# Layer 2's last norm: mean and variance summed by ACT instead of DVE's statistics

## The chip, the cores and the metric

One NeuronCore of a Trainium2 chip runs the whole program. The metric is the device time of one execution in microseconds; lower is better. The engines are PE (matrix products, with its weight loads shown apart as PEld), DVE (vector), ACT (scalar and activation), POOL (GpSimd) and SP (which here issues all transfers).

## The reference

64 matrices of 256 x 128 pass through four layers. All share one 256 x 256 adjacency matrix, and each layer ends with the same residual norm:

```
def _layernorm(x, axis=-1, eps=1e-5):
    m = jnp.mean(x, axis=axis, keepdims=True)
    v = jnp.var(x, axis=axis, keepdims=True)
    return (x - m) / jnp.sqrt(v + eps)
...
x = _layernorm(x + _L0_gnn_ref(...))   # 5 gated steps: adj @ h, three gates, h updated
x = _layernorm(x + _L1_gnn_ref(...))   # two products with weights, mixed by a softmax over the edges
x = _layernorm(x + _L2_gnn_ref(...))   # attention over adj, norm, adj @ h, two-layer MLP with a norm
x = _layernorm(x + _L3_gnn_ref(...))   # Chebyshev: powers of adj times x times weights
```

Layer 2 has norms inside; the one this document is about is its last, over `x + relu(mlp + gat)`: for each of the 256 x 64 rows the mean and variance of 128 numbers, then `(x - m) * (v + eps)^-0.5`. Everything is fp32.

## The kernel before

The 64 matrices are worked in 32 *pairs*. A pair's activations are one tile of 128 partitions x 512: four blocks of 128 tokens x 128 features ("four tiles" of a norm are these blocks, `tokens(v)[:, c, :]`). Products with the adjacency are "spreads" (`spread`, L542, plain; `spread7`, L553, with seven block products in place of eight, whose sums DVE or POOL make at L572 to L574, L581, L585, L587). Between a spread and a weight product the tile may have to be turned (tokens against features): `turn` (L514) does it either by DVE's 32 x 32 transpose and a round trip through DRAM (L529, L531, L537), or by four PE transposes (L523) and a copy out of PSUM. Which of the two is taken is set per site by `BY_DMA` (L18): the last so many pairs of a site are turned by PE.

The order of work is not written out by hand. Every operation is added to a `Schedule` (L102) with the engines it may run on ("ways", each with an assumed duration), what it reads and what it writes. `order` (L132) then plans all 32 pairs at once, greedily: of all operations that are ready it takes the one that can start first, and among those the one that is latest against its due time; for an operation with several ways it takes the engine on which it would end first, after adding a handicap per engine from `SPARE` (L49). Tiles come from fixed classes with a count each (`CLASSES`, L41): a value gets a tile when its first operation is planned, and an operation that finds none free waits. So a change of one assumed duration, one handicap or one count reshuffles the orders of all engines.

The norms are of two sorts. `scale_norm` (L672), used where the mean is already zero, sums the squares by ACT (L645, `Square` with `accum_out`) or by DVE's bn_stats and bn_aggr (L639, L641). `layer_norm` (L626), used at the end of layers 0 and 2, needs mean and variance: `stats` (L591) gets both from DVE's bn_stats and bn_aggr (L600, L602), POOL adds eps and takes the power -0.5 (L605, L608), DVE makes minus mean times that (L610), and `normalize` (L613) applies both, half by half, on DVE (L617) or ACT (L622).

In layer 2 the last steps are: the turn of z, `products` with w2 (L721) on top of a bank seeded with the residual, `y = max(t, 0) + x2` on DVE (L810), `layer_norm(y, x2)` (L812). Layer 3 then turns the result (L529 and on) and spreads it, L827 and L828 multiply both by the weights, L835 multiplies one half by the squared adjacency, L645 to L667 make the last norm, and the result goes out (L841). `x_N` in the profile are the tiles that hold a pair's x through all layers.

Of the kernel before, what the change touches and what calls it, by code (L numbers as in the profile page):

```python
# [8 lines left out]
AF = mybir.ActivationFunctionType  # L9
ALU = mybir.AluOpType  # L10
# [4 lines left out]
D = 128  # L15
STEPS = 5

BY_DMA = {"h": 1, "y": 2, "x1": 0, "x2": 2, "w": 0, "z": 3, "x3": 0}  # L18

WARM = 4  # L20

# [16 lines left out]
ROWS = ["l1_bias", "bp", "b1", "gat_g", "gat_b", "b2"]  # L38


CLASSES = {"X": (512, 15), "T": (512, 4), "A": (512, 30), "H": (520, 6), "B": (1024, 6), "S": (32, 64), "PS": (512, 8), "D": (512, 4), "E": (1024, 8)}  # L41

SEEN = {"PE": 0.23, "ACT": 0.16, "DVE": 0.16, "POOL": 0.12, "SP": 0.0}

# [1 line left out]

AGAIN = {"DVE": 0.12, "POOL": 0.12}

SPARE = {"DVE": 1.0, "DVE+": 0.0, "POOL": -0.3}  # L49


DUE, LAST_DUE, LAST = 15.0, 12.0, 12
# [49 lines left out]
class Schedule:  # L102
# [29 lines left out]
    def order(self, tiles):  # L132
# [14 lines left out]
        while ready:  # L147
            best = None
            for op in ready:
# [7 lines left out]
                for engine, us, fn in op.ways:  # L157
                    us = us if engine == "PE" else us * MARGIN
                    start = max(op.ready, held, *(engines[e] for e in USES.get(engine, (engine,))))
                    end = start + us + SPARE.get(engine, 0.0)  # L160
                    if way is None or end < way[0]:
# [41 lines left out]
def kernel(ctx: ExitStack, tc: tile.TileContext, x, xT, adj, adjT, mats, cols, rows, out):  # L203
    nc = tc.nc
# [5 lines left out]
    S = Schedule(n_pairs)  # L210
# [7 lines left out]
    def act(us, fn, r, w):  # L218
        S.add([("ACT", us, fn)], r, w)

    def dve(us, fn, r, w):
        S.add([("DVE", us, fn)], r, w)
# [4 lines left out]
    def pool(us, fn, r, w):  # L227
        S.add([("POOL-", us, fn)], r, w)
# [103 lines left out]
    for it in range(2):  # L332
        dve(TT, lambda it=it: nc.vector.tensor_tensor_scan(cum.at(2, N)[:, it, :], ones.ap, edge.at(2, N)[:, it, :], 0.0,
                                                            op0=ALU.mult, op1=ALU.add), [edge, ones], [cum])
# [11 lines left out]
    for it in range(2):  # L346
        dve(0.45, lambda it=it: nc.vector.scalar_tensor_tensor(
            num.at(2, N)[:, it, :], cum.at(2, N)[:, it, :], first()[:, it:it + 1], edge.at(2, N)[:, it, :],
            op0=ALU.add, op1=ALU.mult), [cum, small, edge], [num])
        dve(0.35, lambda it=it: nc.vector.tensor_scalar(rowk.at(2, N)[:, it, :], kf.ap, last()[:, it:it + 1], None,  # L350
                                                        op0=ALU.is_lt), [kf, small], [rowk])
        dve(0.45, lambda it=it: nc.vector.scalar_tensor_tensor(
            rowk.at(2, N)[:, it, :], kf.ap, first()[:, it:it + 1], rowk.at(2, N)[:, it, :],
            op0=ALU.is_ge, op1=ALU.mult), [kf, small, rowk], [rowk])
# [13 lines left out]
    for kt in range(2):  # L368
        dve(0.4, lambda kt=kt: nc.vector.tensor_scalar(colk.at(2, N)[:, kt, :], t1.at(2, N)[:, kt, :], kc.ap[:, kt:kt + 1], None,
                                                       op0=ALU.is_equal), [t1, kc], [colk])  # L370
# [7 lines left out]
    for kt in range(2):  # L378
        dve(0.4, lambda kt=kt: nc.vector.tensor_scalar(erow.at(2, N)[:, kt, :], t2.at(2, N)[:, kt, :], col(f"e{kt}"), None,
                                                       op0=ALU.mult), [t2, ccol], [erow])  # L380
# [18 lines left out]
    for it in range(2):  # L399
        act(0.7, lambda it=it: nc.scalar.activation(lg.at(2, N)[:, it, :], lg.at(2, N)[:, it, :], AF.Exp,  # L400
                                                    bias=nmax()[:, it:it + 1], accum_out=den()[:, it:it + 1]), [lg, small], [lg, small])
    dve(0.2, lambda: nc.vector.reciprocal(den(), den()), [small], [small])
    dg = fixed([2, P], "dg")
    for it in range(2):
        blk = lambda it=it: lg.at(2, N)[:, it, it * P:(it + 1) * P]
        dve(0.35, lambda it=it: nc.vector.tensor_scalar(lg.at(2, N)[:, it, :], lg.at(2, N)[:, it, :], den()[:, it:it + 1], None,
                                                        op0=ALU.mult), [lg, small], [lg])
# [95 lines left out]
    def tokens(v):  # L503
        return v.at(4, D)
# [6 lines left out]
    def by_dma(site):  # L511
        return S.pair < n_pairs - BY_DMA[site]

# [74 lines left out]
                                                blk(sv, 0)[:, None, :].to_broadcast([P, 2, P])), [t, p1], [o])  # L588
        return o

    def stats(y, eps=None):  # L591

        s = Value("S", name="mv")
        mv = lambda: s.at(32)[:, 0:8].rearrange("p (t k) -> p t k", k=2)
        rs = lambda: s.at(32)[:, 8:12]
        st = Value("S", name="st")

        def fn():
            for c in range(4):
                nc.vector.bn_stats(st.at(4, 6)[:, c, :], tokens(y)[:, c, :])  # L600
            for c in range(4):
                nc.vector.bn_aggr(mv()[:, c, :], st.at(4, 6)[:, c, :])  # L602
        dve(1.07, fn, [y], [st, s])
        if eps is None:
            pool(0.23, lambda: nc.gpsimd.tensor_scalar(rs(), mv()[:, :, 1], LN_EPS, None, op0=ALU.add), [s], [s])  # L605
        else:
            pool(0.23, lambda: nc.gpsimd.tensor_tensor(rs(), mv()[:, :, 1], eps.at(4), op=ALU.add), [s, eps], [s])
        pool(1.02, lambda: nc.gpsimd.tensor_tensor(rs(), rs(), neg_half.ap, op=ALU.pow), [s, neg_half], [s])  # L608
        nmr = lambda: s.at(32)[:, 12:16]
        dve2(0.08, lambda: nc.vector.scalar_tensor_tensor(nmr(), mv()[:, :, 0], -1.0, rs(), op0=ALU.mult, op1=ALU.mult), [s], [s])  # L610
        return s, rs, nmr

    def normalize(y, o, s, rs, nmr):  # L613
        for half in ((0, 1), (2, 3)):
            def by_dve(half=half):
                for c in half:
                    nc.vector.tensor_scalar(tokens(o)[:, c, :], tokens(y)[:, c, :], rs()[:, c:c + 1], nmr()[:, c:c + 1],  # L617
                                            op0=ALU.mult, op1=ALU.add)

            def by_act(half=half):  # L620
                for c in half:
                    nc.scalar.activation(tokens(o)[:, c, :], tokens(y)[:, c, :], AF.Identity, bias=nmr()[:, c:c + 1],  # L622
                                         scale=rs()[:, c:c + 1])
            S.add([("ACT", 0.78, by_act), ("DVE" if y.cls == "PS" else "DVE+", 0.52, by_dve)], [y, s], [o])

    def layer_norm(y, o):  # L626
        normalize(y, o, *stats(y))

    def scale_stats(ts, eps=None):

# [46 lines left out]
    def layer0(x0, hT):  # L677
        h = x0
        for s in range(STEPS):
            mT = spread7(h, aT, aT7) if s in FAST and FIRST <= S.pair < n_pairs - FINAL else to_sbuf(spread(h, aT), "mT")  # L680
            t = bank()

            def reset(t=t, hT=hT, mT=mT):
                nc.tensor.matmul(t.at(512), mat("u3"), hT.at(512), start=True, stop=False)  # L684
                nc.tensor.matmul(t.at(512), w4.ap, mT.at(512), start=False, stop=True)  # L685
            pe(mm(1024), reset, [Wg, w4, hT, mT], [t])
            r, z, new = (Value("A", name=n) for n in ("r", "z", "hT"))
            act(0.59, lambda t=t, r=r: nc.scalar.activation(r.at(512), t.at(512), AF.Tanh, bias=bzrh.ap[:, 1:2], scale=0.5),  # L688
                [t, bzrh], [r])
            dve2(TT, lambda r=r, hT=hT: nc.vector.scalar_tensor_tensor(r.at(512), r.at(512), 1.0, hT.at(512),  # L690
                                                                      op0=ALU.add, op1=ALU.mult), [r, hT], [r])
            pe(mm(512), lambda t=t, mT=mT: nc.tensor.matmul(t.at(512), w3.ap, mT.at(512), start=False, stop=True,  # L692
                                                            skip_group_check=True), [w3, mT, t], [t])
            act(0.59, lambda t=t, z=z: nc.scalar.activation(z.at(512), t.at(512), AF.Tanh, bias=bzrh.ap[:, 0:1], scale=0.5),  # L694
                [t, bzrh], [z])
            t = bank()

            def candidate(t=t, mT=mT, r=r):
                nc.tensor.matmul(t.at(512), w5.ap, mT.at(512), start=True, stop=False)  # L699
                nc.tensor.matmul(t.at(512), u5h.ap, r.at(512), start=False, stop=True)  # L700
            pe(mm(1024), candidate, [w5, u5h, mT, r], [t])

            act(0.59, lambda t=t: nc.scalar.activation(t.at(512), t.at(512), AF.Tanh, bias=bzrh.ap[:, 2:3]), [t, bzrh], [t])  # L703
            dve(TT, lambda t=t, hT=hT: nc.vector.tensor_sub(t.at(512), t.at(512), hT.at(512)), [t, hT], [t])
            dve(TT, lambda t=t, z=z: nc.vector.scalar_tensor_tensor(t.at(512), z.at(512), 1.0, t.at(512),  # L705
                                                                   op0=ALU.add, op1=ALU.mult), [t, z], [t])
            dve(TT, lambda t=t, hT=hT, new=new: nc.vector.scalar_tensor_tensor(
                new.at(512), t.at(512), 0.5, hT.at(512), op0=ALU.mult, op1=ALU.add), [t, hT], [new])
            hT = new
            h = turn(hT, "h", "h" if s < STEPS - 1 else "y")  # L710
        y = Value("A", name="y")
        dve2(TT, lambda: nc.vector.tensor_add(y.at(512), h.at(512), x0.at(512)), [h, x0], [y])
        layer_norm(y, x0)

    def products(lefts, rights, t=None):

# [25 lines left out]
    def layer2(x2):  # L742
        xT = turn(x2, "xT", "x2")
        h = Value("H", name="h2")
        hs = lambda: h.at(4, D + 2)
        for b in range(2):
            t = Value("PS", name="ps")

            def fn(b=b, t=t):
                for i in range(2):  # L750
                    nc.tensor.matmul(t.at(2, D + 2)[:, i, :], tokens(xT)[:, 2 * b + i, :], wpx.ap, start=True, stop=True)  # L751
# [5 lines left out]
        u, s = Value("B", name="u"), Value("S", name="nm")  # L757
# [7 lines left out]
        for c in range(4):  # L765
            dve2(0.35, lambda c=c: nc.vector.tensor_tensor_reduce(
                out=u.at(4, N)[:, c, :], in0=sd.at(2, N)[:, c // 2, :], in1=maskb.ap[:, c % 2, :], scale=1.0, scalar=-NEG_MASK,
                op0=ALU.add, op1=ALU.max, accum_out=nm()[:, c:c + 1]), [sd, maskb], [u, s])
# [5 lines left out]
        for c in range(4):  # L774
            act(0.4, lambda c=c: nc.scalar.activation(u.at(4, N)[:, c, :], u.at(4, N)[:, c, :], AF.Prelu,
                                                       bias=hs()[:, c, D:D + 1], alpha=0.2), [u, h], [u])
        for c in range(4):
            act(0.5, lambda c=c: nc.scalar.activation(u.at(4, N)[:, c, :], u.at(4, N)[:, c, :], AF.Exp,
                                                       bias=nm()[:, c:c + 1], accum_out=den()[:, c:c + 1]), [u, s], [u, s])
        for b in range(2):  # L780
            half = lambda b=b: u.at(4, N)[:, 2 * b:2 * b + 2, :]
# [5 lines left out]
        for b in range(2):  # L787
# [15 lines left out]
        t, z = seed((0.49, 0.61), tokens, lambda: row("b1", 4), [rbc, gT]), Value("A", name="z")  # L803
# [4 lines left out]
        t, y = seed((0.49, 0.61), tokens, lambda: tokens(hb), [hb, zT]), Value("A", name="y")  # L808
        products([zT], [lambda: mat("w2")], t)
        dve(TT, lambda t=t: nc.vector.scalar_tensor_tensor(y.at(512), t.at(512), 0.0, x2.at(512), op0=ALU.max, op1=ALU.add),  # L810
            [t, x2], [y])
        layer_norm(y, x2)  # L812

    def layer3(x3, p):
        xT = turn(x3, "xT", "x3")
# [37 lines left out]
    tiles = {}  # L853
    for cls, (n, count) in CLASSES.items():
        where = {"PS": psum, "D": dram, "E": dram}.get(cls, shared)
# [46 lines left out]
```

## Time and profile before

| | |
|---|---|
| median of 4 runs | 1487.67 us (1487.22 to 1487.75) |
| the profiled execution | 1487.75 us |
| its span, first to last instruction | 1486.0 us |
| granted PE clock | 1.000 |
| transfers | 146 GB/s on average, 70.8% of 16 engines' time |
| instructions | 28119 |

The profiled execution's own time is 1.75 us longer than its span. How to read the rows: a group's row gives line, engine and operation, output and inputs by the program's tile names, shapes and count, then the busy time in us and the mean ns of one, then how long the engine had been idle before them and what ended the wait. [...]neighbours overlap, so what an operation occupies is the distance between two starts. fp32 matmuls leave two MATMUL records each, transposes one.

### The profile page before, as it was taken

How to read it: one execution, taken by the hardware profiler on the slowest of the kernel's cores; microseconds unless marked ns; L12 is line 12 of the kernel's file. 1: busy time of each engine (PE TensorE's matmuls, PEld its weight loads, DVE VectorE, ACT ScalarE, POOL GpSimd, SP SyncE). 2: the span in 40 equal slices, each digit the busy share in tenths (PEclk: the TensorE clock that was granted, in tenths of full speed). 3: DMA queues.
4: the chain of work that ended last, by engine and by line, in shares of the span. 5: the costliest groups of instructions: out<-in, count | busy, mean ns of one | idle time of the engine just before them, and what ended most of it. 6: DMA issues, size and time to landing. Idle time of an engine off the chain costs nothing.

```text
span 1486.0 us, 28119 instructions
## 1 busy us (share of the span) xinstructions
PE 1475.4 (99%) x7704; PEld 1063.3 (72%) x7704; DVE 1235.9 (83%) x3083; ACT 1027.7 (69%) x3116; POOL 831.1 (56%) x1307
## 2 busy tenths in 40 slices
PE   9999999999999999999999999999999999999998
PEld 6556666666676677777767677777676776788997
DVE  7767888988999899888888888878888888989872
ACT  3444556677777687876786767676686767878875
POOL 4512444555576776664556556565454746676542
PEclk9999999999999999999999999999999999999999
DMA  8544465777788988886778668777777776667862
GB/s 239 121 84 100 100 133 122 144 149 151 157 155 167 177 172 170 160 161 132 150 149 179 133 135 173 153 160 144 148 160 148 151 152 126 135 136 145 170 120 71
DMA packets 946844, 216.60 MB, mean 146 GB/s; under 512 B 726016, under 2 KB 942208, under 8 KB 946688
## 3 DMA queue, kind: packets, MB, share of 16 engines
q1 hardware_dynamic: 946688, 214.81, 70.8%
q8 instruction: 62, 1.02, 0.3%
q14 instruction: 94, 0.77, 0.2%
HBM read 116.86 MB, written 97.85 MB: 144 GB/s over the span
## 4 chain that ended last, share of the span: by engine, by line
PE 97%; DMA 1%; DVE 1%; SPq 0%; ACT 0%; issue 0%; POOLq 0%; ACTq 0%; POOL 0%; DVEq 0%
PE ps L566 24%; PE ps L684 9%; PE ps L685 9%; PE ps L692 9%; PE ps L699 9%; PE ps L700 9%; PE ps L721 7%; PE ps L791 4%; PE ps L835 4%; PE ps L828 4%; PE ps L827 4%; PE ps L548 3%; PE ps L751 2%; DMA e<-a 0%; SPq L537 0%; PE ps L523 0%
## 5 line engine op out<-in xcount | busy, mean ns | idle before, releaser
L566 PEld LDWEIGHTS ps<-aT,a 128*128 128x128 f32 x2144 | 291.4, 192 | 83.4 <-issue 76.1
L236 ACT COPY a<-ps 128x128 f32<-128x128 f32 (+2 forms) x553 | 230.6, 434 | 138.2 <-PE ps L566 49.1
L566 PE MATMUL ps<-aT,a 128*128 128x128 f32 x2144 | 315.5, 275 | 1.0 <-DMA a<-e 0.6
L585 POOL TENSOR_TENSOR a<-a 128x128 f32<-128x128 f32 x205 | 103.8, 510 | 151.8 <-DVE a L581 127.2
L688 ACT ACTIVATE a<-ps,bzrh 128x512 f32<-128x512 f32 x160 | 110.1, 688 | 104.0 <-PE ps L685 89.3
L703 ACT ACTIVATE ps<-ps,bzrh 128x512 f32<-128x512 f32 x160 | 106.1, 663 | 105.7 <-PE ps L700 105.0
L699 PE MATMUL ps<-a,w 128*128 128x512 f32 x320 | 163.6, 593 | 0.0
L700 PE MATMUL ps<-a,u5h 128*128 128x512 f32 x320 | 163.4, 592 | 0.0
L685 PE MATMUL ps<-a,w 128*128 128x512 f32 x320 | 163.4, 592 | 0.0
L692 PE MATMUL ps<-a,w 128*128 128x512 f32 x320 | 162.8, 593 | 0.0
L645 ACT ACTIVATE a<-ps 128x128 f32<-128x128 f32 x488 | 129.1, 283 | 46.4 <-PE ps L721 21.8
L529 DVE STREAM_TRANSPOSE a<-a 128x512 f32<-128x512 f32 x215 | 149.6, 700 | 10.9 <-DMA e<-a 3.1
L587 DVE TENSOR_TENSOR a<-ps,a 128x256 f32<-128x256 f32 x234 | 96.5, 416 | 70.1 <-ACT a L236 32.8
L721 PE MATMUL ps<-W,a 128*128 128x128 f32 x1024 | 144.4, 275 | 0.0
L721 PEld LDWEIGHTS ps<-W,a 128*128 128x128 f32 x1024 | 132.8, 192 | 16.1 <-issue 13.9
L653 POOL TENSOR_TENSOR s<-s,neg_half 128x4 f32<-128x4 f32 x128 | 138.9, 1085 | 7.6
L694 ACT ACTIVATE a<-ps,bzrh 128x512 f32<-128x512 f32 x160 | 110.6, 691 | 44.6 <-PE ps L692 37.4
L684 PE MATMUL ps<-a,W 128*128 128x512 f32 x256 | 131.0, 593 | 0.0
L685 PEld LDWEIGHTS ps<-a,w 128*128 128x128 f32 x320 | 60.8, 190 | 76.5 <-issue 68.2
L700 PEld LDWEIGHTS ps<-a,u5h 128*128 128x128 f32 x320 | 60.8, 190 | 76.5 <-issue 63.8
L705 DVE SCALAR_TENSOR_TENSOR ps<-a,ps 128x512 f32<-128x512 f32 x160 | 109.7, 686 | 6.1 <-ACT a L694 4.4
L581 POOL TENSOR_TENSOR a<-a 128x256 f32<-128x256 f32 x99 | 73.8, 748 | 70.0 <-ACT a L236 69.6
(208 smaller groups left out, 3326.1 us busy)
## 6 DMA issues: line engine op xcount, KB each, us to landing
e<-a SPq DMA_DIRECT2D x277, 256.0 KB
a<-e SPq DMA_DIRECT2D x1108, 64.0 KB
e<-b SPq DMA_DIRECT2D x32, 512.0 KB
b<-e SPq DMA_DIRECT2D x128, 128.0 KB
x<-x_in SPq DMA_DIRECT2D x32, 256.0 KB
t<-xT_in SPq DMA_DIRECT2D x32, 256.0 KB
a<-d SPq DMA_DIRECT2D x32, 256.0 KB
y_out<-a SPq DMA_DIRECT2D x32, 256.0 KB
```

The lines of the kernel that those rows point to most:

```text
L236: S.add([("ACT", us[0], lambda: nc.scalar.copy(o(), i())), ("DVE", us[1], lambda: nc.vector.tensor_copy(o(), i()))], r, w)
L529: dve(n / 512 * 0.55 + 0.09, lambda: nc.vector.transpose(st.at(n), i.at(n)), [i], [st])
L566: pe(mm(128), lambda: nc.tensor.matmul(blk(t, k), left(), rt(), start=start, stop=True, skip_group_check=True), [*r, right, terms, *[t] * ...
L645: nc.scalar.activation(tokens(junk)[:, c, :], v.at(len(tiles), D)[:, k, :], AF.Square, scale=D ** -0.5, accum_out=mv()[:, c, 1:2])
L653: pool(1.02, lambda: nc.gpsimd.tensor_tensor(rs(), rs(), neg_half.ap, op=ALU.pow), [s, neg_half], [s])
L684: nc.tensor.matmul(t.at(512), mat("u3"), hT.at(512), start=True, stop=False)
L685: nc.tensor.matmul(t.at(512), w4.ap, mT.at(512), start=False, stop=True)
L692: pe(mm(512), lambda t=t, mT=mT: nc.tensor.matmul(t.at(512), w3.ap, mT.at(512), start=False, stop=True, skip_group_check=True), [w3, mT, t ...
L694: act(0.59, lambda t=t, z=z: nc.scalar.activation(z.at(512), t.at(512), AF.Tanh, bias=bzrh.ap[:, 0:1], scale=0.5), [t, bzrh], [z])
L699: nc.tensor.matmul(t.at(512), w5.ap, mT.at(512), start=True, stop=False)
L700: nc.tensor.matmul(t.at(512), u5h.ap, r.at(512), start=False, stop=True)
L721: nc.tensor.matmul(tokens(t)[:, c, :], tokens(i)[:, c, :], w(), start=(first and k == c == 0), stop=(k == len(lefts) - 1), skip_group_chec ...
```

## The change

`stats` gets a flag `by_act`, true for layer 2 and false for layer 0. With it, four ACT operations of two tiles each take the place of L600 and L602: two with `Identity`, whose accumulator gives the mean (scaled by 1/128), and two with `Square`, scaled by 128^-0.5 and with minus the mean, scaled alike, as bias, whose accumulator gives the variance. A small multiply by -128^-0.5 on ACT or POOL makes the bias in between. The element results go to `o`, which `normalize` overwrites later. Four constants change with it: pairs turned by PE at two sites, the number of B tiles (attention weights), and the planner's handicaps for DVE.

```diff
-BY_DMA = {"h": 1, "y": 2, "x1": 0, "x2": 2, "w": 0, "z": 3, "x3": 0}
+BY_DMA = {"h": 1, "y": 0, "x1": 0, "x2": 3, "w": 0, "z": 3, "x3": 0}
...
-CLASSES = {"X": (512, 15), "T": (512, 4), "A": (512, 30), "H": (520, 6), "B": (1024, 6), "S": (32, 64), "PS": (512, 8), "D": (512, 4), "E": (1024, 8)}
+CLASSES = {"X": (512, 15), "T": (512, 4), "A": (512, 30), "H": (520, 6), "B": (1024, 5), "S": (32, 64), "PS": (512, 8), "D": (512, 4), "E": (1024, 8)}
...
-SPARE = {"DVE": 1.0, "DVE+": 0.0, "POOL": -0.3}
+SPARE = {"DVE": 0.6, "DVE+": 0.2, "POOL": -0.3}
...
-    def stats(y, eps=None):
+    def stats(y, o, by_act, eps=None):
...
-        dve(1.07, fn, [y], [st, s])
+
+        def sums(k, func, bias):
+            for half in ((0, 1), (2, 3)):
+                def fn(half=half):
+                    for c in half:
+                        nc.scalar.activation(tokens(o)[:, c, :], tokens(y)[:, c, :], func, scale=D ** (k / 2 - 1),
+                                             accum_out=mv()[:, c, k:k + 1], **bias(c))
+                act(0.57, fn, [y, *[st] * k], [s, o])
+        if by_act:
+            sums(0, AF.Identity, lambda c: {})
+            S.add([("ACT", 0.2, lambda: nc.scalar.mul(st.at(4), mv()[:, :, 0], -D ** -0.5)),
+                   ("POOL-", 0.23, lambda: nc.gpsimd.tensor_scalar(st.at(4), mv()[:, :, 0], -D ** -0.5, None, op0=ALU.mult))], [s], [st])
+            sums(1, AF.Square, lambda c: {"bias": st.at(4)[:, c:c + 1]})
+        else:
+            dve(1.07, fn, [y], [st, s])
...
-    def layer_norm(y, o):
-        normalize(y, o, *stats(y))
+    def layer_norm(y, o, by_act):
+        normalize(y, o, *stats(y, o, by_act))
...
-        layer_norm(y, x0)
+        layer_norm(y, x0, False)
...
-        layer_norm(y, x2)
+        layer_norm(y, x2, True)
```

## The prediction

> **What bounds the kernel now.** I read the page's busy times first, then a table of busy times by stretch of 50 us, then groups of instructions by line, and last the order of time around the end.
>
> ```profile
> span 1486.0 us, 28119 instructions
> PE 1475.4 (99%) x7704; PEld 1063.3 (72%) x7704; DVE 1235.9 (83%) x3083; ACT 1027.7 (69%) x3116; POOL 831.1 (56%) x1307
> ```
>
> PE is busy for 1475.4 of 1486.0 us; all other engines have room. The time can move only by PE's work or by the 10.6 us in which PE stands. The table by stretch tells where these lie (span, then busy us and instructions of PE, PEld, DVE, ACT, POOL, granted clock, DMA share, GB/s). Outside the five stretches shown PE is busy 50.00 of 50.00:
>
> ```profile
> 0.00:50.00 50.00, 48.80 (x186) 31.48 (x187) 37.33 (x94) 19.52 (x32) 27.41 (x53) 1.00 0.80 217
> ...
> 450.00:500.00 50.00, 48.27 (x272) 34.41 (x270) 45.54 (x118) 35.99 (x109) 34.62 (x53) 1.00 0.94 177
> 500.00:550.00 50.00, 49.64 (x283) 37.62 (x283) 45.65 (x123) 39.81 (x131) 37.57 (x57) 1.00 0.80 165
> ...
> 1350.00:1400.00 50.00, 49.01 (x332) 44.79 (x331) 45.37 (x147) 44.03 (x174) 32.12 (x46) 1.00 0.77 155
> ...
> 1450.00:1486.00 36.00, 29.70 (x141) 25.27 (x140) 6.89 (x22) 18.23 (x73) 9.41 (x15) 0.98 0.30 74
> ```
>
> Idle: 1.20 at the start, 1.73 + 0.36 around 470 to 500 us (the stretch with the highest DMA share, 0.94), 0.99 near 1364, 6.30 at the end. The chain of waits puts the last matmul's end at 1480.05, so 5.9 of the 6.30 is the last norm and its output, which the change leaves alone. What a better order could win back is 1.73 + 0.36 + 0.99 + 0.4 = 3.5 us. A busy record hides some more: a 128-column MATMUL is recorded as 275 ns, yet in a dense stretch such records start 0.11 us apart, so each gap is up to 0.16 us deeper than the table says. Over some 20 visible gaps that is 3 us more, 6.5 in all.
>
> **What the Trainium skill says.** "Perfetto Trace Analysis", section "Tensor Engine Instruction (MATMUL, LD_WEIGHTS)": a matmul's end is computed, not observed; the 275 against 111 ns above agrees, so I use distances between starts. The same section calls ACT, DVE and GpSimd strict FIFOs, so a long block on ACT delays whatever is queued behind it; no view of before contradicts it. "ScalarE: Activation LUTs", section "What ACT_TABLE_LOAD costs": an ACTIVATE with immediates takes 186 ns + 0.833 ns per element, each per-partition pointer adds 93 ns, and neighbours overlap by 93 ns. The trace agrees for 128 elements out of SBUF: L622 with two pointers starts every 0.77/2 = 0.385 us, L734 with one every 1.17/4 = 0.29 us:
>
> ```profile
> 710.03 0.87 ACT L622 ACTIVATE x<-a,s 128x128 f32<-128x128 f32 x2
> 710.80 1.27 ACT L734 ACTIVATE a<-x,dcol 128x128 f32<-128x128 f32 x4
> 711.97 0.68 ACT L688 ACTIVATE a<-ps,bzrh 128x512 f32<-128x512 f32 x1
> ```
>
> **The change part by part.** The comparison of instruction orders shows how the planner reshuffles everything, so I count engine by engine.
>
> *PE.* BY_DMA "y" 2 to 0 takes two PE turns away (8 transposes), "x2" 2 to 3 adds one (4). Net 4 transposes fewer. In the chain of waits four of L523 take 0.44 us: **-0.44 us** on the bound itself. No other matmul changes in number.
>
> *DVE.* 128 of the 256 bn_stats and bn_aggr leave:
>
> ```profile
> L600 DVE BATCH_NORM_STATS2 s<-a 128x6 f32<-128x128 f32 x256 | 54.8, 275 | 0.3
> L602 DVE BATCH_NORM_AGGREGATE s<-s 128x2 f32<-128x6 f32 x256 | 23.1, 151 | 0.0
> ```
>
> One norm holds DVE for 1.07 us (1460.99 to 1462.06 below), 32 norms 34 us. The planner refills: L581 135 to 90 and L572 109 to 78 (76 at some 0.36 us between starts, -27), L667 37 to 113 (76 at 0.33, +25), L639 with L641 24 to 62 (38 at 0.27, +10), the rest about -8. Net -34 us: 83% falls to 81%.
>
> *ACT.* Per norm four Identity sums without pointers (estimate: 0.29 less one pointer's 0.093 = 0.20, and 0.09 for the accumulator read, as the second starts of L645 show: 0.29), four Squares with one pointer (0.29 + 0.09 = 0.385), and for 20 of 32 norms the 128x4 multiply. The trace has no such multiply on ACT; from below 0.10 (the skill's 186 + 3 - 93 ns), from above 0.25 (L665's distance); I take 0.1. Sum 1.16 + 1.54 + 0.1 = 2.8 us, x32 = 90 us. Back come 38 L645 and 152 L665 at 0.25 (-47) and 13 large copies (-6); 12 L622 and 5 relus come in (+7). Net +44 us: 69% rises to 72%. All of it lies beside PE's work, unless it makes PE wait.
>
> *POOL.* +76 L572/L581 at 0.75 to 0.8 us, 12 multiplies, others: about +80 us, 56% to 61%. Hidden too.
>
> *The norm's latency.* Here is the last pair's way from its last layer 2 product (L721 ends at 1460.17) on:
>
> ```profile
> 1460.27 0.69 DVE L810 SCALAR_TENSOR_TENSOR a<-ps,x 128x512 f32<-128x512 f32 x1 [3.89 <-PE ps L721]
> 1460.99 0.87 DVE L600 BATCH_NORM_STATS2 s<-a 128x6 f32<-128x128 f32 x4
> 1461.78 0.36 DVE L602 BATCH_NORM_AGGREGATE s<-s 128x2 f32<-128x6 f32 x4
> 1462.06 0.39 DVE L667 TENSOR_TENSOR a<-ps,s 128x256 f32<-128x256 f32 x1
> ...
> 1462.23 0.23 POOL L605 TENSOR_SCALAR s<-s 128x4 f32<-128x4 f32 x1 [1.43 <-DVE s L602]
> 1462.54 1.03 POOL L608 TENSOR_TENSOR s<-s,neg_half 128x4 f32<-128x4 f32 x1
> ...
> 1465.58 0.37 SPq L531 DMA_DIRECT2D e<-a  x1
> 1467.94 1.92 SPq L537 DMA_DIRECT2D a<-e  x4
> ```
>
> Statistics take 1.15 us from y to the aggregate's end. On ACT they are 2.8 us plus three handovers of about 0.1: 3.1, so **2.0 us longer** on a chain of dependencies that ends in the turn. Within a stage many pairs are in flight, and PE has other pairs' matmuls. At the end there is no such cover: before, the way from L721's end to the turned x is about 12 us (DMA issue ends 1469.86, about 2 us landing), and PE's order has 13.8 us of other matmuls there. In the changed order I count 15.6 us of matmuls between the same two points (12.2 up to the last plain spread, 1.7 for it, 1.7 for a L835 group). The new way needs 12 + 2.0 = 14.0, and up to 15.6 if ACT is still busy with the four L645 and four L665 queued ahead of the last sums (about 1.6 us after y is ready). So the tail is covered, just; I book 0 there, 1 us in the bad case.
>
> *Turns and pools.* "y" by DMA for the last two pairs costs a DMA round trip of some 6 us in place of about 1 us on PE and ACT; pairs 30 and 31 still have three layers of others' work around them then. 0, at most 1. One B tile less keeps fewer attention weights in flight; the trace has no price for it; 0 to 2 us of PE waits, I take 0. SPARE moves choices only, counted above.
>
> **Sum, against the profiled execution:** 1486.0 span and 1487.75 us, 1.75 outside the span. -0.44 for PE; and I expect PE's waits of 3.5 to 6.5 us, which came from a few late transfers and one bank, to come out near their old size in other places (DVE less loaded: -0.7). 1487.75 - 0.44 - 0.7 = 1486.6; the median of runs is 0.08 below the profiled one, so **1486.5**.
>
> **Rivals.**
> 1. *As forecast*, 1483.5 to 1490: no stage's bound changes. For it: PE at 50.00 in 25 of 30 stretches with three engines below 85%. Against it: every buffer and queue is reordered, and an order with so few gaps is easy to lose. Chance 0.47.
> 2. *The waits go*: DVE's relief lets the late copies and turns come in time, and 3 to 6.5 us of PE waits vanish: 1487.67 - 0.44 - 4.5 = 1482.7. For it: DVE is the second busiest engine, at 45.5 of 50 where the waits are. Against it: the largest of these follow a load of x and turns that took 4.2 and 3.8 us to land in the densest DMA stretch, which no statistics on ACT make faster. 0.21.
> 3. *ACT in the way, slower.* Place: the sums come as blocks of four tiles, 1.2 and 1.5 us, on a strict FIFO that also evacuates each spread (L236, 0.59 us) between its first and second products. In both orders, 5% of these spreads leave PE no more than 2.2 us of other matmuls there; the copy and its handovers need about 0.75, so 1.4 us of slack. A block of 1.5 us in front, with ACT already a little late, eats it. Price: of about 225 spreads in the kernel 11 are so tight; at 0.5 us each, 5.5 us: 1492. If also POOL's extra 80 us makes second sums (L585, L581) late, double that, 1497. It decides from 3.4 us net on. For it: ACT at 44.03 of 50 in 1350 to 1400 already, where the planner packs pairs closer. Against it: elsewhere ACT is at 32 to 41 of 50, and copies waiting for PE (49.1 us of L236 idle before L566) rather than PE for copies. 0.32.
> 4. *It doesn't do what it says*: excluded by the order, where 128 Identity and 128 Square stand on ACT and half of L600 and L602 are gone.
>
> **How the numbers follow.** About 0.2%, 3 us, can be told from no change: 1484.7 to 1490.6. Rival 2 and nothing else is faster: 0.22; rival 3 gives slower: 0.33; the middle 0.45. The range from 1483 to 1497 takes in rival 2 down to its middle and rival 3 up to its doubled price; the likeliest case alone is 1483.5 to 1490.
>
> **What would show it.** Right: PE's busy sum about 1475.0 with idle gaps of 2 to 8 us before the tail; the ACT sums starting 0.29 and 0.385 us apart; ACT near 72%, DVE near 81%, POOL near 61%; the last product waiting under 1 us for its turned x. Wrong: PE waits on ACT L236 behind blocks of sums adding up to several us (rival 3); PE busy 50.00 in all stretches from 450 to 1400 (rival 2); a wait of over 2 us between the last plain spread and its product, which would say that the norm's longer chain was not covered.

## The result and the profile after

| | median | runs | ratio to before, 95% interval |
|---|---|---|---|
| before | 1487.86 us | 51 | |
| changed | 1490.66 us (1488.57 to 1493.5) | 31 | 1.0019 [1.0014, 1.0024] |

The change makes the kernel slower by 0.19%, 2.8 us. That is a difference of the size that was called "no change" beforehand, but the runs tell it from zero, and the forecast had a gain of 1.2 us. The changed kernel's profiled execution took 1489.4 us, at the low end of its runs, while the one of before (1487.75) was near its median. So these two traces differ by only 1.7 us, and the rest of the 2.8 cannot be seen in them.

The page's busy times of the changed kernel:

```profile
span 1487.6 us, 28259 instructions
...
PE 1475.6 (99%) x7700; PEld 1062.1 (71%) x7700; DVE 1212.0 (81%) x2886; ACT 1063.1 (71%) x3422; POOL 899.1 (60%) x1410
```

The shift of work came much as counted: DVE's busy time is 24 us less, ACT's 35 more, POOL's 68 more, and PE has 4 matmuls fewer. PE is still the bound, and PE's waits have grown. The table by stretch of 50 us (columns as before), with the five stretches of most idle PE:

```profile
0.00:50.00 50.00, 48.80 (x203) 33.12 (x204) 38.81 (x101) 20.82 (x37) 28.56 (x54) 1.00 0.65 178
...
300.00:350.00 50.00, 48.90 (x250) 32.84 (x249) 43.45 (x90) 30.46 (x86) 33.05 (x51) 1.00 0.77 153
...
1050.00:1100.00 50.00, 49.56 (x266) 35.81 (x265) 42.29 (x114) 40.72 (x142) 28.07 (x45) 1.00 0.72 150
...
1350.00:1400.00 50.00, 47.49 (x315) 43.44 (x315) 42.24 (x127) 45.65 (x193) 35.67 (x51) 1.00 0.68 144
1450.00:1486.00 36.00, 31.47 (x154) 26.93 (x152) 10.63 (x30) 21.09 (x96) 10.08 (x16) 0.98 0.35 80
```

The waits near 470 to 500 us are almost gone (2.09 to 0.14 us in 450 to 550), but 1350 to 1400 has 2.51 us in place of 0.99, and 300 to 350 has 1.10 in place of 0. Counted from start to start of all matmuls, which also finds what the record ends hide, with the median distance of each shape in the kernel before as the usual one, PE's excess is 9.9 us against 8.0 before, and the usual distances sum to 1470.0 us against 1470.5. The 0.4 us from the transposes were gained; 1.9 us more of waits were lost.

In the worst stretch, ACT's order of time shows one norm's sums and what stands behind them:

```profile
1358.59 0.33 ACT L608 ACTIVATE x<-a 128x128 f32<-128x128 f32 x1
...
1358.88 0.33 ACT L608 ACTIVATE x<-a 128x128 f32<-128x128 f32 x1
...
1361.70 0.20 ACT L613 ACTIVATE s<-s 128x4 f32<-128x4 f32 x1
1361.81 0.25 ACT L236 COPY a<-ps 128x128 f32<-128x128 f32 x1
1361.96 0.40 ACT L608 ACTIVATE x<-a,s 128x128 f32<-128x128 f32 x1
...
1362.35 0.39 ACT L608 ACTIVATE x<-a,s 128x128 f32<-128x128 f32 x1
...
1363.51 1.05 ACT L236 COPY a<-ps 128x512 f32<-128x512 f32 x2
```

Starts lie 0.29 us apart for Identity and 0.39 for Square, and the small multiply occupies 0.11: the prices of the forecast hold. The four Squares run from 1361.96 to 1363.51 with two copies of spreads (L236) queued behind them. PE's waits of the same stretch, longest in total first (engine, tile and line, then who released it: us, times, longest):

```profile
PEld ps L566 <- ACT a L236: 1.3, 1, 1.3
PEld ps L841 <- DVE a L587: 0.8, 1, 0.8
PEld ps L566 <- ACT a L813: 0.7, 1, 0.7
PEld ps L548 <- ACT a L679: 0.7, 1, 0.7
```

The longest one ends at 1364.60, with the second of those two copies. That is the picture of the slower rival. But a wait seen behind a block does not show that the wait would go without the block, and a planner has reordered everything around it; hence the experiments.

### The profile page after: what moved, and what is told of

It reads as the page before. It is cut to its first block, busy times and chain, and to the rows that moved or that the text cites. A ratio compares the mean times of both kernels' runs of the same rounds, so it can differ in the third digit from the quotient of the medians.

```text
span 1487.6 us, 28259 instructions
## 1 busy us (share of the span) xinstructions
PE 1475.6 (99%) x7700; PEld 1062.1 (71%) x7700; DVE 1212.0 (81%) x2886; ACT 1063.1 (71%) x3422; POOL 899.1 (60%) x1410
## 4 chain that ended last, share of the span: by engine, by line
PE 94%; DVE 2%; ACT 1%; SPq 1%; DMA 1%; issue 1%; POOL 0%; POOLq 0%; ACTq 0%; DVEq 0%
PE ps L566 23%; PE ps L713 9%; PE ps L699 9%; PE ps L714 9%; PE ps L698 9%; PE ps L706 9%; PE ps L735 7%; PE ps L849 4%; PE ps L805 4%; PE ps L841 4%; PE ps L842 4%; PE ps L548 2%; PE ps L765 2%; SPq L537 1%; ACT x L608 0%
## 5 line engine op out<-in xcount | busy, mean ns | idle before, releaser
L566 PEld LDWEIGHTS ps<-aT,a 128*128 128x128 f32 x2144 | 291.4, 192 | 81.6 <-issue 71.2
L236 ACT COPY a<-ps 128x512 f32<-128x512 f32 (+2 forms) x542 | 225.6, 429 | 136.6 <-PE ps L566 42.9
L566 PE MATMUL ps<-aT,a 128*128 128x128 f32 x2144 | 314.8, 275 | 0.1
L702 ACT ACTIVATE a<-ps,bzrh 128x512 f32<-128x512 f32 x160 | 109.9, 687 | 94.2 <-PE ps L699 80.6
L581 POOL TENSOR_TENSOR a<-a 128x256 f32<-128x256 f32 x144 | 108.1, 755 | 111.6 <-ACT a L236 108.0
L659 ACT ACTIVATE a<-ps 128x128 f32<-128x128 f32 x450 | 119.1, 282 | 39.4 <-PE ps L735 16.8
L572 POOL TENSOR_TENSOR a<-a 128x256 f32<-128x256 f32 x95 | 72.4, 763 | 90.0 <-DMA a<-e 54.4
```

Source lines behind the costliest of these rows:

```text
L236: S.add([("ACT", us[0], lambda: nc.scalar.copy(o(), i())), ("DVE", us[1], lambda: nc.vector.tensor_copy(o(), i()))], r, w)
L566: pe(mm(128), lambda: nc.tensor.matmul(blk(t, k), left(), rt(), start=start, stop=True, skip_group_check=True), [*r, right, terms, *[t] * ...
L659: nc.scalar.activation(tokens(junk)[:, c, :], v.at(len(tiles), D)[:, k, :], AF.Square, scale=D ** -0.5, accum_out=mv()[:, c, 1:2])
```

## The experiments

Three theories were held, the third only after the first set. **A**: the sums on ACT delay what is queued behind them. **B**: the new order that the four constants bring costs the time, and the sums matter little. **C**: every change of any number makes the planner draw a new order of everything, PE's waits are a matter of that draw, and the kernel before is a good draw. A "draw" here is one such plan, and a kernel is "redrawn" when a number is changed that asks for no other work. Differences to the kernel before are to its runs of the same set (medians 1487.51, 1486.79 and 1487.10 us in the three sets).

### First set: each half of the change, with a new plan and with the old one

`const_only` calls `layer_norm(y, x2, False)` in the changed kernel. `act_only` keeps the sums and takes the four constants back:

```diff
-BY_DMA = {"h": 1, "y": 0, "x1": 0, "x2": 3, "w": 0, "z": 3, "x3": 0}
+BY_DMA = {"h": 1, "y": 2, "x1": 0, "x2": 2, "w": 0, "z": 3, "x3": 0}
...
-SPARE = {"DVE": 0.6, "DVE+": 0.2, "POOL": -0.3}
+SPARE = {"DVE": 1.0, "DVE+": 0.0, "POOL": -0.3}
```

(and six B tiles).

> The four changed constants stay, layer 2's statistics go back to DVE. If the sums on ACT cost the time (theory A: blocks of sums in ACT's queue make copies and seeds late, PE waits for them), the loss of 2.8 us goes: 1487 to 1488.5 us, ratio 0.9995 to 1.0005 to the kernel before, and PE's waits on ACT near 1355 to 1372 us are gone. If a reshuffled order with these constants costs it (theory B: any new order of all engines opens new gaps, the sums matter little), it stays at 1490 to 1492, ratio 1.0015 to 1.003.

> The sums on ACT with the four constants of the kernel before. Theory A: as slow as the changed kernel or slower, 1490.5 to 1493 us, since the constants were not what cost. Theory B: the constants carried the loss, so 1487 to 1489 us, ratio within 0.001 of 1.

Measured: const_only 1499.05 us, 1.0073 [1.0061, 1.0085]; act_only 1493.04 us, 1.0035 [1.0022, 1.0048]. Neither half alone is the loss: the plan with the constants alone is 11.5 us slower, the one with the sums alone 5.5, the one with both 2.8. Nothing adds up here: const_only misses both A and B by 7 us and more, act_only lies at the upper edge of A, and the two halves can't be priced by planning them apart.

The other two keep an order and swap only the engine under it. `order_after_dve` plans the changed kernel but issues DVE's statistics where the first Identity stands, and nothing for the rest:

```diff
+            none = lambda: None
+            act(0.57, fn, [y], [s, o])
+            act(0.57, none, [y], [s, o])
...
```

`order_before_act` plans the kernel before and issues the eight sums in the place of its statistics (`o` is given for layer 2 alone):

```diff
...
-        dve(1.07, fn, [y], [st, s])
+        dve(1.07, sums if o is not None else fn, [y], [st, s])
```

> The changed kernel's plan and its order of all other instructions, but DVE's bn_stats and bn_aggr are issued at the place of the first Identity sum, and ACT's eight sums, its reads and the small multiply are left away. Only ACT's load changes (some 90 us less) and DVE's (34 us more). Theory A: PE's waits on late ACT work shrink, in the profile the 3.2 us near 1360 to 1371 us to under 1 us, and the time falls by 2 to 3 us to 1487.5 to 1488.7. Theory B: the gaps lie in the order itself, 1490 to 1491.5.

> The kernel before with its plan and order, but at the place of DVE's statistics in layer 2 ACT does the eight sums and the small multiply, which the plan knows nothing of (2.8 us of ACT 32 times, and each norm 2 us later). Theory A: the order has no room for it on ACT, so PE waits grow: 1491 to 1497 us. Theory B: ACT at 69% has room, 1487.5 to 1489.

Measured: order_after_dve 1494.36 us, 1.0046 [1.0034, 1.0058]; order_before_act 1528.23 us, 1.0273 [1.026, 1.0286]. Work that the plan doesn't know of is dear on either engine: 34 us of it on DVE cost 3.7 us over the changed kernel, although ACT was relieved of some 90; about 90 us of it on ACT cost 40. So order_after_dve did not isolate ACT's part, as I had meant it to: it took one load away and put another, unplanned one in.

### Second set: is it the draw?

Four controls change a number that asks for no other work: the planner's factor on durations from 1.1 to 1.102, or the distance of due times from 15.0 to 15.02.

```diff
-MARGIN, LAG = 1.1, 0.3
+MARGIN, LAG = 1.102, 0.3
```

> A control: the kernel before with the planner's factor on durations at 1.102 in place of 1.1. It asks for no other work, but some 5,000 lines of PE's order differ. Theory C (the time of one plan is a draw: each small change of any number redraws where PE waits, and the kernel before is a good draw): slower than before by 2 to 12 us, 1490 to 1499. Theory A and B (a cause in the sums or in one constant): a number without meaning changes nothing, 1486.5 to 1489.

> A second control of the same sort: due times 15.02 us apart in place of 15.0. Theory C: 1490 to 1499 us, and another value than the first control's. Theories A and B: 1486.5 to 1489.

> The changed kernel with the factor at 1.102. Theory C: the changed kernel is a good draw as well, so slower than it, 1491 to 1500, within the same band as the redrawn kernel before. Theory A: the sums on ACT cost in any plan, so the redrawn changed kernels lie above the redrawn ones of before by 2 us and more.

> The changed kernel with due times 15.02 us apart. Theory C: 1491 to 1500. Theory A: above the redrawn kernels before by 2 us and more. If the ACT sums are a gain that the two drawn plans hide, both redrawn changed kernels lie below both redrawn kernels before.

| | us | ratio to before, 95% interval |
|---|---|---|
| before_margin | 1492.98 | 1.0040 [1.0027, 1.0052] |
| before_due | 1490.24 | 1.0022 [1.0015, 1.0030] |
| after_margin | 1492.40 | 1.0037 [1.0024, 1.0051] |
| after_due | 1500.22 | 1.0086 [1.0073, 1.0100] |

Theory C holds for what it says of draws (after_due is even a little above its band). A change in the third or fourth digit costs the kernel before 3.5 or 6.2 us, and the changed one some 2.7 or 10 us by the ratios (1.0037 and 1.0086 against 1.0019). The kernel before is faster than all redrawn ones, and so is the changed kernel within its own family. Theory A's test in this set failed: after_margin does not lie above both redrawn kernels before. Two draws in each family don't tell which mean is lower.

One part of what these plans lose does go with the sums. It is a wait before the last turned x (`L841 <- DMA a<-e`, 24 matmuls from the end), the place where the forecast had looked for the norm's longer chain. By distances between starts it is 1.3 us in act_only, 2.2 in after_margin and 2.6 in after_due, and 3.4 in `priced` below. The changed kernel itself has none, nor have the four plans with DVE's statistics: before, before_margin, before_due and const_only. (order_after_dve, an order planned for the sums, has 1.1 us there.) That the longer norm causes it is likely, but no run takes the sums out of one of these plans.

### Third set: the same order, less or more work in it

Here PE's, DVE's, POOL's and SP's orders are those of the changed kernel to the line, and only ACT's sums are taken out or doubled; in the third, DVE's statistics are taken out of the order of before.

after_sums_out:

```diff
-                    for c in half:
-                        nc.scalar.activation(tokens(o)[:, c, :], tokens(y)[:, c, :], func, scale=D ** (k / 2 - 1),
-                                             accum_out=mv()[:, c, k:k + 1], **bias(c))
+                    if k == 0 and half == (0, 1):
+                        nc.scalar.activation(s.at(32)[:, 0:8], y.at(512)[:, 0:8], AF.Square)
```

after_sums_twice:

```diff
-                    for c in half:
+                    for c in (*half, *half):
```

before_stats_out (`out` is true for layer 2 alone):

```diff
...
-        dve(1.07, fn, [y], [st, s])
+        dve(1.07, (lambda: nc.vector.tensor_mul(s.at(32)[:, 0:8], y.at(512)[:, 0:8], y.at(512)[:, 0:8])) if out else fn, [y], [st, s])
```

> The changed kernel's order kept on PE, DVE, POOL and SP to the line; on ACT the eight sums of each norm are left out and one Square of 8 numbers writes the eight statistics in their place, so layer 2's last norm gets wrong statistics. It frees some 2.6 us of ACT per norm, 84 us in all, and shortens each norm by as much. Theory A (the sums are what makes PE wait in this plan): 1487.5 to 1488.7 us, the whole 2.8 us come back. Theory C (PE's waits belong to the drawn plan as a whole): 1489.5 to 1491, the waits near 1360 to 1371 us stay or move.

> The changed kernel's order kept, each of the eight sums done twice: 2.7 us more of ACT per norm, 86 us in all, which the plan doesn't know of. Theory A: linear, another 3 us and more, 1493 to 1497. Theory C: the first 2.7 us were planned and this is not, so it is far dearer than the first, 1500 us and more (90 unplanned us in the kernel before cost 40).

> The kernel before with its order kept; DVE's statistics of layer 2 are left out and one product of 8 numbers stands in their place, so that norm gets wrong statistics. It frees 1.0 us of DVE per norm, 32 us in all, at no cost to ACT: the most that the change can bring DVE. If DVE's load makes PE wait, 1484 to 1486 us. If not (theory C), 1486.5 to 1488.

Measured: after_sums_out 1487.64 us, 0.9998 [0.9990, 1.0007]; after_sums_twice 1530.64 us, 1.0294 [1.0280, 1.0308]; before_stats_out 1487.68 us, 1.0002 [0.9994, 1.0010].

The first and the third give A and C one point each: after_sums_out lies where A put it and below C's band, before_stats_out where C put it; after_sums_twice is far above A's linear estimate, as C expected. Together they answer two questions that replanning can't. **Within the plan that was drawn, the sums cost as much as the whole loss**: without them the same order runs as fast as the kernel before. And **no gain from DVE's relief is seen**: with its 32 us gone at no cost to ACT, in an order that was not planned anew, the kernel before measures 0.3 us slower, with an interval from 0.9 faster to 1.5 slower. The page of before_stats_out shows DVE at 81% and PE's work where it was.

```profile
PE 1474.9 (99%) x7704; PEld 1063.3 (72%) x7704; DVE 1209.6 (81%) x2859; ACT 1028.0 (69%) x3116; POOL 828.1 (56%) x1307
```

The stretch 1355 to 1372 us of the changed kernel, from its table by stretch, and then the same of after_sums_out (whose work there lies some 1 to 1.5 us earlier):

```profile
1355.00:1372.00 17.00, 14.49 (x100) 12.95 (x99) 15.59 (x41) 16.32 (x68) 13.15 (x18) 1.00 0.75 162
```

```profile
1355.00:1372.00 17.00, 15.74 (x108) 14.08 (x107) 15.26 (x44) 14.65 (x56) 13.91 (x20) 1.00 0.82 178
```

ACT's busy time falls by 1.67 us, from 16.3 of 17, and PE's idle time by 1.25 us, from 2.51 to 1.26. Of the waits listed above, the two that change most are L566 behind its copy (L236) and L548 behind L679; in after_sums_out, by its list of waits for this stretch:

```profile
PEld ps L566 <- ACT a L813: 0.8, 1, 0.8
PEld ps L841 <- DVE a L587: 0.8, 1, 0.8
PEld ps L566 <- ACT a L236: 0.5, 1, 0.5
PEld ps L548 <- ACT a L679: 0.2, 1, 0.2
```

The two others stay to a tenth: they belong to the order, not to the sums. The rest of the 3.0 us between the medians is not in this stretch, and not all of it is in the traces, whose spans differ by 1.5 us. Over the whole run, PE's excess of more than 0.15 us at a start, put to what released the matmul or its weights, was:

| us | behind ACT | behind DVE |
|---|---|---|
| before | 2.5 | 1.9 |
| changed | 3.5 | 3.5 |
| after_sums_out | 1.6 | 3.3 |

So taking the sums out shortens the waits behind ACT and hardly those behind DVE: it is ACT that had been late, as theory A has it. But after_sums_out is not the kernel before again. Its order waits longer behind DVE and less behind ACT than that kernel's, and comes out even.

In order_after_dve, PE idles for as much as 2.1 us in the same stretch without any sum on ACT, with DVE close to full:

```profile
1355.00:1372.00 17.00, 14.90 (x104) 13.37 (x103) 16.28 (x51) 12.64 (x51) 11.45 (x19) 1.00 0.68 152
```

So DVE's statistics put in there unplanned fill DVE to 16.3 of 17. PE's longest wait there, 1.2 us, is for a copy by ACT, but that copy had itself waited 1.35 us for DVE, where statistics stood in front of its input.

Doubled, the same sums cost 40 us. Their first 2.7 us per norm, which the plan had places for, cost 0.09 us per norm (3.0 us over 32 norms, changed kernel less after_sums_out, give or take 1.5); the next 2.7 us, which it had none for, cost 1.25 us per norm. The three longest groups of PE's waits for ACT in after_sums_twice, over the whole run (in the changed kernel the first is 3.6 us and the third, for the seeding copy, 0.2):

```profile
PEld ps L566 <- ACT a L236: 14.2, 18, 3.4
...
PEld ps L706 <- ACT a L702: 7.9, 6, 2.5
PEld ps L735 <- ACT ps L236: 7.1, 9, 1.9
```

Each is work of ACT that PE's next matmuls wait for: the copy of a spread's first products out of PSUM, an activation in layer 0's gates (L702), and the seed of a bank.

One more run gave the planner the sums' measured durations:

```diff
-                act(0.57, fn, [y, *[st] * k], [s, o])
+                act((0.54, 0.70)[k], fn, [y, *[st] * k], [s, o])
```

> The changed kernel with the planner's price of the sums set to what the changed kernel's trace shows: 0.54 for two Identity sums and 0.70 for two Squares (times the factor 1.1: 0.59 and 0.77) in place of 0.57 for either. Theory A: a plan that knows the true length has room for it, 1486 to 1489. Theory C: one more draw, 1490 to 1500.

Measured: 1502.27 us, 1.0095 [1.0082, 1.0109]. A truer price did not give a better kernel; it gave another draw, above even C's band, with two PE waits of 3.4 and 3.6 us near its end:

```profile
PEld ps L841 <- issue: 3.6, 1, 3.6
PEld ps L548 <- ACT b L792: 3.4, 1, 3.4
```

The first of them is again the wait before the last turned x. No version that was run beats the kernel before.

## Why the prediction was wrong

- **The bound**: right. PE bounds all kernels here, and what is lost is lost in PE's waits (in some of the slower plans also in stretches of half clock, see the last section).
- **PE's own work**, -0.44 us: right; the usual distances sum to 0.45 us less.
- **DVE, ACT and POOL**: right in direction and near in size (-24, +35, +68 us of busy time, for -34, +44, +80, of which DVE's and ACT's were counted by distances between starts). The prices of Identity, Square and the small multiply (0.29, 0.385, 0.1) came out at 0.29, 0.39 and 0.11. The pricing rule that was taken from the Trainium skill ("ScalarE: Activation LUTs", "What ACT_TABLE_LOAD costs") thus held in this trace for an ACTIVATE with an accumulator read, once the read's 0.09 was added.
- **"All of it lies beside PE's work, unless it makes PE wait"**: this is the step that failed. I booked ACT's 90 us at 0 since ACT as a whole would rise only from 69% to 72%. In the drawn plan they cost some 3 us, shown by taking them out with every other engine's order kept. The share over the run hid stretches like 1355 to 1372, where ACT is at 96%. This is rival 3, right in mechanism (copies and other work of ACT late behind the sums) and about twice too high in price (5.5 us). The same slip is in rival 1's "three engines below 85%": it holds for the whole run, but before the change DVE was at 47.88 of 50 us from 400 to 450.
- **"DVE less loaded: -0.7"**: not shown. before_stats_out has no gain from freeing DVE, but its interval, from 0.9 us faster to 1.5 slower, takes in -0.7. Nor does it show what a plan could make of the free time.
- **"PE's waits come out near their old size"**: the second term that failed. They grew by 1.9 us in the trace, and that they grew no more was luck of the draw: eight new plans lie 2.8 to 15 us above the kernel before (changed kernel, const_only, act_only, the four controls, priced). I had written that an order with so few gaps is easy to lose, and left it out of the sum; by these eight it should have been the centre of the forecast, with a loss of several us.
- **The norm's longer latency at the end**, booked at 0: right for this plan, by luck. After the last spread the longest excess is 0.19 us, and L841 does not wait. In all four other plans with the sums on ACT it does, for 1.3 to 3.4 us, so the cover of 15.6 us of matmuls was this plan's and not a property of the change, and "1 us in the bad case" was too little.
- **"y", "x2", the B tiles and SPARE**: booked at 0. They can't be priced one by one in this kernel, because each alters the draw; the one plan that has all of them without the sums is 11.5 us slower.

Open: whether layer 2's sums on ACT would be better than DVE's statistics on the average of many plans. Two redraws of each family can't tell, and no more were made; the wait before the last turned x is the one cost that was seen to come back.

## What to carry to other kernels

Where one planner orders everything, compare plans, not edits: first measure how far the time moves when a number without meaning is changed, and take no step smaller than that as the edit's own. To price an edit itself, keep the order to the line and take the work out, or double it. An engine at 70% over the whole run may have no room in the stretch that counts, and relief for an engine that does not set the time may bring nothing that can be measured.

## What was not expected of the hardware

In the traces of six of the slower kernels PE's clock was granted at half for 3.4 us in the middle of the run or near its end, while matmuls were still to come; in the kernel before and the changed one, whose longest mid-run waits are 1.0 and 1.3 us, it is at half only after the last matmul. In const_only, PE waits for 2.2 us near 1405 us; the table by stretch of 4 us shows the granted clock after it (column before the last two):

```profile
1404.00:1408.00 4.00, 1.79 (x15) 1.57 (x15) 3.97 (x16) 3.37 (x19) 2.23 (x3) 1.00 1.27 220
1408.00:1412.00 4.00, 4.00 (x25) 4.00 (x24) 3.14 (x7) 1.50 (x10) 3.59 (x7) 0.59 0.73 158
1412.00:1416.00 4.00, 3.53 (x28) 3.29 (x28) 3.26 (x13) 4.00 (x15) 2.24 (x4) 0.98 0.95 220
```

In that stretch 128-column matmuls start 0.21 us apart, in place of 0.11. So in 3.4 us PE does 1.7 us less work, and a wait of about 2 us that is followed by one costs nearly twice its length. after_due, after_margin, priced, order_before_act and after_sums_twice have one to two such stretches each (in after_due the first is 6.8 us long).

The length of the wait alone does not decide: 2.2 us brought half clock in const_only, 2.5 us near 1412 us in before_due did not. The traces show what does. Wherever a run has more than one switch to half, the switches lie whole multiples of 3.413 us apart (in priced 1421.98, 1486.83 and 1497.07 us: 19 and 3 times). Cut these six runs, and the others on the grid of their switch at the end, into windows of that length and count PE's idle time in each by distances between starts: in the window just before a stretch at half it was 2.09 to 3.39 us, and in all windows that nothing followed it was at most 2.11. (before_due's wait falls across two windows, with 1.7 and 0.9 us.) So in these runs the border lies near 2.1 us of idle time in one window of 3.41. In the changed kernel's trace no window with the matmuls under way has more than 1.5 us. It is part of why the slow plans are as slow as they are; the loss that the changed kernel's trace shows has none of it.
